# Turning the normed tokens of self-attention in two partition groups, two feature chunks at a time

## The chip, the cores and the metric

The kernel runs on one core of a Trainium2 chip, as one launch. The metric is the device time of that launch in microseconds (us); smaller is better. The core has a matrix engine (TensorE, called PE in the profile, with its weight loads shown as PEld), a vector engine (VectorE, DVE), a scalar engine (ScalarE, ACT), a general engine (GpSimd, POOL) and a queue that issues transfers (SyncE, SP). Each engine works through its own list of instructions in order and waits for the others through semaphores. Matrix products land in PSUM, which is used here in banks of 512 numbers for each of 128 partitions; all other tiles lie in SBUF.

## The reference

One transformer block on 16 batches of 224 tokens with 512 features, all in float32:

```
shift_a, scale_a, gate_a, shift_m, scale_m, gate_m = split(silu(c) @ W_mod + b_mod, 6)
x_norm = ln(x) * (1 + scale_a) + shift_a
q, k, v = split(x_norm @ W_qkv + b_qkv, 3)               # 16 heads of 32 features
x = x + gate_a * (softmax(q k' / sqrt(32)) v @ W_proj + b_proj)
... cross-attention: queries from ln(x), keys and values from ln(context), 750 tokens ...
h = gelu((ln(x) * (1 + scale_m) + shift_m) @ W_mlp1 + b_mlp1)
x = x + gate_m * (h @ W_mlp2 + b_mlp2)
```

The change touches the step from `ln(x)` to `x_norm` in the first line of self-attention. A product contracts over the partitions, so the features of `x_norm` must lie on the partitions, while the normed tokens come with tokens on the partitions. They are turned on PE.

## The kernel before, in words

The kernel runs three stages one after the other: self-attention over all batches, cross-attention, and the MLP. Instructions are emitted in an order written out by hand (class `Ordered` keeps program order on every engine); the tile pools decide which physical buffer a tile gets and put in the waits. All instructions are recorded under line 28, so the profile's groups are told apart by tile names.

Self-attention works on pairs of batches (`PB = 2`, eight pairs p), and in a pair on eight units: four groups g of four heads, for each batch j of the pair. A unit u = 2g + j is a pass of the loop at lines 627 to 642: `self_scores` (products `sc<-qk`, then a DVE maximum `m<-sc` and its split into three bf16 parts, `nm`), the close of an earlier unit (`finish`: DVE reciprocal and product into `at`), planned work of slot 0, `self_weights` of the unit before (`sc<-mrow,ones` and `sc<-qk`, then one ACT exponential into `pt`), `max_rows` (two PE transposes of `nm` and a DVE copy into `mrow`), `add_keys` (a DVE sum `acc`), planned work of slot 1, and `self_values` (`o<-pt,v`, `o<-acc,ones`).

Planned work of pair p prepares pair p + 1. In units 1 and 2 the next pair's tokens are normed (`xn`, written by POOL). Unit 4 holds, in slot 0, the query projection `project_qk(p, 3)` and the turning of chunks 0 and 1; in slot 1, the key projection `project_qk(p, KC + 3)` and the turning of chunks 2 and 3 (lines 551 and 552). Units 5 and 6 hold the value projections of the next pair, unit 7 its first query and key projections. Before the loop, pair 0 is turned by lines 616 and 617. So the turning happens once ahead of the loop and seven times within it.

A chunk k is 128 of the 512 features. `transpose_pair` (lines 310 to 318) turns one chunk of a pair: four transposes, one for each 112 tokens of the 448, into one PSUM bank, then two DVE steps (`modulate`, lines 304 to 308), one for each batch, that multiply and add the per-feature scale and shift while they copy 224 columns from PSUM into `xt`. In a transpose the tokens are the loaded weights and the identity matrix streams past them, so one transpose streams as many columns as it has token rows.

The banks for all of this, for the projections and for `max_rows` come from one pool of three (`ps_mm`, line 234), named `mm` in the profile and handed out in turn. A new tile waits until the last reader of the tile three places earlier is done. In unit 4 the order is: query projection (bank A), chunk 0 (B), chunk 1 (C), `max_rows` (A, free when DVE has moved the query projection out into `qk`), key projection (B, free when chunk 0 is modulated), chunk 2 (C), chunk 3 (A). ACT moves the key projection out.

`Unit.maxima` of cross-attention (lines 1026 to 1046) already turns a tile of 125 rows in two groups of 64 and 61 rows, into two banks; its instructions are called `mm<-ident,top`.

Of the kernel before, what the change touches and what calls it, by code (L numbers as in the profile page):

```python
# [8 lines left out]
F32 = mybir.dt.float32  # L9
# [28 lines left out]
def kernel(  # L38
# [24 lines left out]
    B, N, H = x.shape  # L63
    S = context.shape[1]
    MLP = w_mlp1.shape[1]
    P = 128
    NH = 16
    HD = H // NH
    KC = H // P
    NF = MLP // P  # L70
    HG = P // HD
    TP = 112
    TC = N // TP
    CP = 125
    CC = S // CP
    CH = CC // 2
    RG = 64
    PB = 2
    NP = B // PB
    PT = PB * TC  # L80
    HS = CH * CP
    PN = PB * N
    GB = 4
# [15 lines left out]
    ident = const.tile([P, P], F32, name="ident")  # L99
# [14 lines left out]
    for i in range(3):  # L114
        t = const.tile([TP, TC, HG, HD], BF16, name=f"nm{i}")
# [35 lines left out]
    def load_x(pool, src, bufs):  # L151
        t = pool.tile([TP, TC, H], F32, name="x", bufs=bufs)
        nc.sync.dma_start(out=t, in_=src)
        return t

    def tokens(dram_x, b):
        return dram_x[b].rearrange("(c p) d -> p c d", p=TP)

    def load_w(pool, w, name, bufs=1):
        kc = w.shape[0] // P  # L160
        t = pool.tile([P, kc, w.shape[1]], F32, name=name, bufs=bufs)
        nc.sync.dma_start(out=t, in_=w.rearrange("(k p) n -> p k n", p=P))
        return t

    mm, turn = nc.tensor.matmul, nc.tensor.transpose
# [73 lines left out]
    def load_part(i):  # L239
        w_part[i] = load_w(mp, w_mod[:, i * H : (i + 1) * H], "w_mod", 2)  # L240
# [3 lines left out]
    load_part(0)  # L244
    for b in range(PB):
        xs[b] = load_x(sa, tokens(x, b), 6)
# [8 lines left out]
    for i in range(2):  # L255
        lo = (2 + 3 * i) * H
# [4 lines left out]
    ps = ps_mm.tile([P, 512], F32, name="mm")  # L261
# [15 lines left out]
    def part_rows(i):  # L277

        ps = ps_mm.tile([P, 512], F32, name="mm")
        for k in range(KC):  # L280
            mm(ps[:B, :H], c_t[:, k, :], w_part[i][:, k, :], start=(k == 0), stop=(k == KC - 1))
        if i % 3 < 2:
            r = mp.tile([B, H], F32, name="part", bufs=2)
            nc.scalar.copy(r, ps[:B, :H])
            return r
        return ps
# [17 lines left out]
    def modulate(psum_ap, dst, b, k, i_shift, i_scale):  # L304
        nc.vector.tensor_scalar(
            dst, psum_ap, mod_t[:, i_scale + k, b : b + 1], mod_t[:, i_shift + k, b : b + 1],
            ALU.mult, ALU.add,
        )

    def transpose_pair(pool, psum, xn, p, i_shift, i_scale, k):  # L310

        ps = psum.tile([P, 512], F32, name="mm")
        for t in range(PT):
            turn(ps[:, t * TP : (t + 1) * TP], xn[t // TC][:, t % TC, k * P : (k + 1) * P], ident[:TP, :TP])
        xt = pool.tile([P, PN], F32, name="xt", bufs=2 * KC)
        for j in range(PB):
            modulate(ps[:, j * N : (j + 1) * N], xt[:, j * N : (j + 1) * N], PB * p + j, k, i_shift, i_scale)
        return xt

# [69 lines left out]
    def halves(products):  # L391

        parts = []

        def first():
            parts.append(products())
            next(parts[0])

        return first, lambda: next(parts[0], None)

    def whole(products):
        for _ in products:
            pass
# [32 lines left out]
    if True:  # L436
# [3 lines left out]
        xts = {}  # L440
# [4 lines left out]
        def project_qk(p, m):  # L445
            ps = ps_mm.tile([P, 512], F32, name="mm")
            for k in range(KC):
                mm(
                    ps[:, :PN], (wq, wk)[m // KC][:, k, (m % KC) * P : (m % KC + 1) * P], xts[p][k],
                    start=(k == 0), stop=(k == KC - 1),  # L450
                )
                if k == 1:
                    yield
            t = sa.tile([P, PN], F32, name="qk", bufs=6)
            bm = bcol[:, o_qkv + m : o_qkv + m + 1]
            if m < KC:
                nc.vector.tensor_scalar(t, ps[:, :PN], bm, SCALE, ALU.add, ALU.mult)
            else:
                nc.scalar.activation(t, ps[:, :PN], AF.Identity, bias=bm)
            qk[p, m] = t  # L460
# [12 lines left out]
        def fetch(p):  # L473
            for b in range(PB * p, PB * (p + 1)):
                xs[b] = load_x(sa, tokens(x, b), 6)
# [6 lines left out]
                )  # L482

        def turn_x(p, k):
            xts.setdefault(p, []).append(
                transpose_pair(
                    sa, ps_mm, [xns[PB * p + j] for j in range(PB)], p, i_shift_a, i_scale_a, k
                )
            )

        def project(p, t):
            b, c = PB * p + t // TC, t % TC
            if c == 0:
                gate[b] = gate_rows(sa, 0, b * N, TP, 2)
            ps = ps_mm.tile([P, 512], F32, name="mm")
            yield from project_heads(ps, at[p], wproj, t * TP)
            add_to_x(sa, ps[:TP, :H], xs[b][:, c, :], bproj, gate[b])
            if c == TC - 1:
                nc.sync.dma_start(out=x_self[b], in_=xs[b])
# [3 lines left out]
        def at_slot(p, u, slot, f):  # L503
            if p < NP:
                plan.setdefault((p, u, slot), []).append(f)

        for p in range(NP):
            if p < NP - 1:
                for g in range(1, KC):
                    at_slot(p, 2 * g - 2, 0, lambda p=p, g=g: whole(project_qk(p, g)))  # L510
                    at_slot(p, 2 * g - 2, 1, lambda p=p, g=g: whole(project_qk(p, KC + g)))
                for t in range(PT if p else 0):
                    at_slot(p, 1 + t // 2 * 2, t % 2, lambda p=p, t=t: whole(project(p - 1, t)))
            else:

                left = [(project_qk, p, m) for m in (1, KC + 1, 2, KC + 2)]
                left += [(project, p - 1, t) for t in range(2)]
                left += [(project_qk, p, m) for m in (3, KC + 3)]
                left += [(project, p - 1, t) for t in range(2, PT)]
                parts = [h for f, *args in left for h in halves(lambda f=f, args=args: f(*args))]  # L520
                for i, h in enumerate(parts):
                    at_slot(p, i // 3, i % 3 // 2, h)
            if p == 0:
                made = {}

                def part(i):
                    made[i] = part_rows(i)
                    if i % 3 == 2:
                        finish_part(i, made[i])

                at_slot(p, 1, 0, lambda: part(2))
                at_slot(p, 1, 1, lambda: part(3))
                at_slot(p, 1, 1, lambda: load_part(4))
                at_slot(p, 1, 1, lambda: load_part(5))
                at_slot(p, 2, 0, lambda: finish_part(3, made[3]))
                at_slot(p, 3, 0, lambda: part(4))
                at_slot(p, 3, 1, lambda: part(5))
                at_slot(p, 3, 1, lambda: finish_part(4, made[4]))
                at_slot(p, 3, 1, load_cross)
            n = p + 1  # L540
            if n < NP:
                if n > 1:
                    at_slot(p, 0, 0, lambda n=n: fetch(n))
                at_slot(p, 1, 0, lambda n=n: norm_begin(n))
                for t in range(PT):
                    at_slot(
                        p, 1 + t // 2, t % 2, lambda n=n, t=t: norms[PB * n + t // TC].stats(t % TC)
                    )
                for j in range(PB):
                    at_slot(p, 1 + j, 1, lambda n=n, j=j: norms[PB * n + j].apply())  # L550
                for k in range(KC):
                    at_slot(p, 4, k // 2, lambda n=n, k=k: turn_x(n, k))
                for t in range(PT):
                    at_slot(p, 5 + t // 2, t % 2, lambda n=n, t=t: project_v(n, t))
                at_slot(p, 7, 0, lambda n=n: whole(project_qk(n, 0)))
                at_slot(p, 7, 1, lambda n=n: whole(project_qk(n, KC)))
# [56 lines left out]
        load_part(3)  # L613
        fetch(1)
        wproj = load_w(ws, w_proj, "wproj")
        for k in range(KC):
            turn_x(0, k)
        whole(project_qk(0, 0))
        whole(project_qk(0, KC))
# [213 lines left out]
    with tc.tile_pool(name="ca", bufs=2, reuse_waits="tile") as ca:  # L833
# [3 lines left out]
        xt = {}  # L837
# [94 lines left out]
        for b in range(B):  # L932
            n = b + 1
# [52 lines left out]
        class Unit:  # L986
# [39 lines left out]
            def maxima(self):  # L1026
# [3 lines left out]
                for s in range(HG):  # L1030
                    for c in range(TC):
                        for i, (r, n) in enumerate(((0, RG), (RG, CP - RG))):
                            lo = (s * TC + c) * n
# [3 lines left out]
                            )  # L1037
                for i, n in enumerate((RG, CP - RG)):
                    m = small.tile([TP, HG, TC], F32, name=f"mc{i}")
# [303 lines left out]
```

## Time and profile before

Three runs took 2906.09, 2906.14 and 2911.99 us, median 2906.14. The profiled execution took 2907.9 us.

| what | value |
|---|---|
| profiled execution, own time | 2907.9 us |
| its span, first to last instruction | 2906.1 us |
| granted TensorE clock | 0.993 |
| PE busy | 2834.6 us, 98% |
| DVE busy | 1926.2 us, 66% |
| POOL busy | 1201.5 us, 41% |
| ACT busy | 1119.7 us, 39% |
| self-attention, from 100 to 690 us | PE busy 582.34 of 590 us, DVE 415.71 us |
| transposes `mm<-ident,xn`, 112 rows, all stages | 248, PE busy 30.0 us |
| steps `xt<-mm,mod_t`, 224 columns | 64, DVE busy 28.1 us, 502 ns for one |

PE is busy nearly all the time in every stage, so what counts is what PE has to do and where it stands still. A mean duration in a row covers one instruction from start to end; neighbours overlap, so the step from one to the next is shorter than the duration and is read from the timeline. An idle time in brackets is that of the engine just ahead of the row, with what released it.

### The profile page before, as it was taken

To read this page: it belongs to the slowest core of one execution; us is meant where nothing else is said; L and a number is where in the kernel's file an instruction comes from. 1 tells how busy PE (TensorE), PEld (TensorE's weight loads), DVE (VectorE), ACT (ScalarE), POOL (GpSimd) and SP (SyncE) were. 2 spreads that over 40 slices of the span, in tenths; PEclk is the share of its full clock that TensorE was granted. 3 is DMA by queue.
4 is the path that set the end of the run, shared out by engine and by line. 5 is a ranking of instruction groups with operands and counts; after the bars stand their busy time and mean duration, and the time that the engine had idled before them with its cause. 6 is when DMAs were issued, how large, how long until landed. Compare 5 with 4: busy or idle time off the path is not lost. (4 is left out here: it accounts for less than half of the span.)

```text
span 2906.1 us, 47040 instructions
## 1 busy us (share of the span) xinstructions
PE 2834.6 (98%) x19733; PEld 1810.3 (62%) x19733; DVE 1926.2 (66%) x2764; ACT 1119.7 (39%) x1402; POOL 1201.5 (41%) x1357
## 2 busy tenths in 40 slices
PE   8999999998999999999999999999979999999999
PEld 3444444444555565555656556556546888888888
DVE  4666776676478778787787787877775643444343
ACT  1222222221356655665566556655643112112211
POOL 1022222122356666676666766666551210221021
PEclk9999999998999999999999999999999999999999
DMA  5111110100100010100101100000013111110110
GB/s 191 59 33 33 32 33 10 60 11 24 57 32 24 23 35 24 35 26 21 35 24 35 35 19 28 27 33 24 22 44 107 55 37 37 44 58 29 45 44 30
DMA packets 55384, 114.43 MB, mean 39 GB/s; under 512 B 4308, under 2 KB 4372, under 8 KB 55172
## 3 DMA queue, kind: packets, MB, share of 16 engines
q1 hardware_dynamic: 54560, 110.58, 11.8%
q8 instruction: 155, 2.54, 0.4%
q10 hardware_dynamic: 612, 0.85, 0.1%
q14 instruction: 57, 0.47, 0.1%
HBM read 89.33 MB, written 22.09 MB: 38 GB/s over the span
## 5 line engine op out<-in xcount | busy, mean ns | idle before, releaser
L28 POOL TENSOR_TENSOR acc<-acc,pt 125x448 f32<-125x448 f32 x504 | 573.6, 1138 | 39.5
L28 ACT COPY pt<-sc 125x1792 f32<-125x1792 f32 x192 | 317.3, 1653 | 563.1 <-DVE top L28 510.1
L28 DVE TENSOR_TENSOR pt<-pt,o 125x896 f32<-125x896 f32 x384 | 394.2, 1081 | 88.1 <-PE o L28 85.5
L28 DVE TENSOR_TENSOR top<-top,sc 125x896 f32<-125x896 f32 x320 | 346.4, 1083 | 35.4 <-PE sc L28 28.7
L28 PE MATMUL mm<-wkvc,cxt 128*125 128x512 f32 x768 | 354.4, 604 | 6.9 <-ACT kt L28 6.9
L28 PE MATMUL mm<-cxt,wkvc 128*128 128x375 f32 x1024 | 355.0, 489 | 2.3 <-ACT cxt L28 2.3
L28 ACT ACTIVATE pt<-pt 125x896 f32<-125x896 f32 x384 | 338.4, 951 | 20.0 <-DVE pt L28 19.4
L28 POOL TENSOR_TENSOR upd<-upd,gate 112x512 f32<-112x512 f32 (+1 forms) x60 | 79.2, 1321 | 632.9 <-DVE upd L28 628.4
L28 POOL TENSOR_TENSOR acc<-pt 125x448 f32<-125x448 f32 x126 | 143.8, 1141 | 447.7 <-ACT pt L28 447.7
L28 PEld LDWEIGHTS mm<-cxt,wkvc 128*128 128x128 f32 x1024 | 185.6, 191 | 119.8 <-issue 16.6
L28 DVE RECIPROCAL at<-o 128x224 f32<-128x224 f32 x128 | 198.6, 1552 | 72.9 <-PE o L28 72.9
L28 PEld LDWEIGHTS mm<-wkvc,cxt 128*125 128x125 f32 x768 | 136.5, 187 | 171.5 <-issue 153.2
L28 ACT ACTIVATE pt<-sc 112x1792 f32<-112x1792 f32 x64 | 106.5, 1663 | 333.8 <-PE sc L28 333.8
L28 POOL TENSOR_TENSOR rstd<-mv,eps 112x2 f32<-112x2 f32 (+3 forms) x93 | 18.0, 193 | 508.8 <-DVE mv L28 508.8
L28 PE MATMUL sc<-qt,kt 32*125 32x224 f32 x3072 | 201.6, 377 | 14.0 <-ACT pt L28 13.4
L28 PE MATMUL mm<-xt,wqkv 128*128 128x448 f32 x512 | 208.6, 550 | 5.7 <-DVE xt L28 4.7
L28 DVE TENSOR_REDUCE m<-sc 112x8 f32<-112x1792 f32 x64 | 129.6, 2025 | 121.8 <-PE sc L28 121.8
L28 PEld LDWEIGHTS sc<-qt,kt 32*125 32x125 f32 x3072 | 133.1, 183 | 94.1 <-issue 33.8
L28 PE MATMUL o<-pt,vt 125*32 125x224 f32 x3072 | 158.6, 354 | 0.0
L28 PEld LDWEIGHTS mm<-xt,wqkv 128*128 128x128 f32 x512 | 92.0, 190 | 87.6 <-issue 80.4
L28 DVE TENSOR_REDUCE mc<-mm 112x8 f32<-112x512 f32 (+1 forms) x128 | 79.8, 665 | 98.3 <-PE mm L28 98.3
L28 ACT COPY mx<-a 128x512 f32<-128x512 f32 x26 | 15.2, 586 | 327.0 <-POOL upd L28 307.9
(185 smaller groups left out, 4656.5 us busy)
## 6 DMA issues: line engine op xcount, KB each, us to landing
cx<-in_ctx_dram SPq DMA_DIRECT2D x96, 250.0 KB
x<-in_x_dram SPq DMA_DIRECT2D x16, 448.0 KB
x_self<-x SPq DMA_DIRECT2D x16, 448.0 KB
x<-x_self SPq DMA_DIRECT2D x16, 448.0 KB
x_cross<-x SPq DMA_DIRECT2D x16, 448.0 KB
mx<-x_cross SPq DMA_DIRECT2D x28, 256.0 KB
w<-in_L_xcond_W_mlp_dram SPq DMA_DIRECT2D x7, 1024.0 KB
xr<-x_cross SPq DMA_DIRECT2D x28, 256.0 KB
```

What stands on the lines that cost most here:

```text
L28: return lambda *args, **kw: self.tc.keep_in_program_order(f(*args, **kw))
```

## The change

`transpose_pair` now turns two chunks in one call and takes two banks for it. The 112 token rows are split into partitions 0 to 63 and 64 to 111 (`ROWS`). For each chunk and each 112 tokens there are two transposes, of 64 and of 48 rows, one after the other in the list, into different banks. A bank so holds, for both chunks, the columns of one row group of all four token blocks. The two chunks take 16 transposes instead of eight. Each bank is then modulated in four steps, one for each chunk and batch: eight steps for two chunks instead of four, of 2 x 64 or 2 x 48 columns instead of 224. Each reads a contiguous run from PSUM and writes two separate runs into `xt`. The order of the steps is: chunk k from the first bank (two steps), chunk k from the second bank (two), then chunk k + 1 in the same way. The plan calls the new function once a slot instead of twice; the slots, the pool and the number of banks stay.

```diff
+    ROWS = (0, RG), (RG, TP - RG)
...
+    def turn_rows(banks, srcs, ks):
+
+        for i, k in enumerate(ks):
+            for t, src in enumerate(srcs):
+                for bank, (r, n) in zip(banks, ROWS):
+                    lo = (i * len(srcs) + t) * n
+                    turn(bank[:, lo : lo + n], src[r : r + n, k * P : (k + 1) * P], ident[r : r + n, r : r + n])
+
     def transpose_pair(pool, psum, xn, p, i_shift, i_scale, k):
 
-        ps = psum.tile([P, 512], F32, name="mm")
-        for t in range(PT):
-            turn(ps[:, t * TP : (t + 1) * TP], xn[t // TC][:, t % TC, k * P : (k + 1) * P], ident[:TP, :TP])
-        xt = pool.tile([P, PN], F32, name="xt", bufs=2 * KC)
-        for j in range(PB):
-            modulate(ps[:, j * N : (j + 1) * N], xt[:, j * N : (j + 1) * N], PB * p + j, k, i_shift, i_scale)
-        return xt
+        banks = [psum.tile([P, 512], F32, name="mm") for _ in ROWS]
+        turn_rows(banks, [xn[t // TC][:, t % TC, :] for t in range(PT)], (k, k + 1))
+        xts = []
+        for i in range(2):
+            xt = pool.tile([P, PN], F32, name="xt", bufs=2 * KC)
+            for bank, (r, n) in zip(banks, ROWS):
+                for j in range(PB):
+                    lo = (i * PT + j * TC) * n
+                    modulate(
+                        bank[:, lo : lo + TC * n].rearrange("p (c t) -> p c t", c=TC),
+                        xt[:, j * N : (j + 1) * N].rearrange("p (c t) -> p c t", c=TC)[:, :, r : r + n],
+                        PB * p + j, k + i, i_shift, i_scale,
+                    )
+            xts.append(xt)
+        return xts
...
-            xts.setdefault(p, []).append(
+            xts.setdefault(p, []).extend(
...
-                for k in range(KC):
+                for k in range(0, KC, 2):
                     at_slot(p, 4, k // 2, lambda n=n, k=k: turn_x(n, k))
...
-        for k in range(KC):
+        for k in range(0, KC, 2):
             turn_x(0, k)
```

## The prediction

> **What bounds the kernel now.** I read the page's busy shares first, then the stretches by stage, then who PE waits for, then the timeline around one turn, and at last rows that price the new shapes. Page and stretches (span; PE, PEld, DVE, ACT, POOL busy):
>
> ```profile
> PE 2834.6 (98%) x19733; PEld 1810.3 (62%) x19733; DVE 1926.2 (66%) x2764; ACT 1119.7 (39%) x1402; POOL 1201.5 (41%) x1357
> ...
> 100.00:690.00 590.00, 582.34 (x4515) 287.85 (x4514) 415.71 (x676) 128.95 (x113) 124.16 (x150) 1.00 0.09 27
> ```
>
> In the stage that the change touches PE is busy 98.7% at the full granted clock, DVE 70%. So time moves where PE gets less work or stands longer. What it waits for from 37 to 690 us (total, times, longest):
>
> ```profile
> PE mm L28 <- DVE xt L28: 4.7, 7, 0.7
> PE mm L28 <- DVE qk L28: 3.7, 8, 0.8
> ```
>
> The first comes seven times: once per turned pair, and it ends with a modulate step of just this change. The timeline of the first of the seven (start, length, idle before):
>
> ```profile
> 87.39 0.93 PE L28 MATMUL mm<-ident,xn 112*128 112x112 f32 x8
> ...
> 88.25 0.40 PE L28 MATMUL sc<-mrow,ones 3*112 3x448 bf16 x4
> ...
> 89.10 0.67 DVE L28 TENSOR_SCALAR qk<-mm,bcol 128x448 f32<-128x448 f32 x1
> ...
> 89.69 1.76 DVE L28 TENSOR_SCALAR xt<-mm,mod_t 128x224 f32<-128x224 f32 x4
> 89.83 0.26 PE L28 MATMUL mm<-ident,nm 112*128 112x112 bf16 x2 [0.42 <-DVE qk L28]
> ...
> 90.76 3.25 PE L28 MATMUL mm<-xt,wqkv 128*128 128x448 f32 x8 [0.67 <-DVE xt L28]
> ...
> 93.84 0.93 PE L28 MATMUL mm<-ident,xn 112*128 112x112 f32 x8
> ...
> 94.43 1.77 DVE L28 TENSOR_SCALAR xt<-mm,mod_t 128x224 f32<-128x224 f32 x4 [1.80 <-PE mm L28]
> 94.70 0.96 PE L28 MATMUL o<-pt,v 112*32 112x224 f32 x16
> ```
>
> To see: in unit 4, DVE runs one chain (maximum, reciprocal, `at`, `qk`, four modulates) and PE waits for it twice, 0.42 us for bank A (`qk` moved out) and 0.67 us for bank B (chunk 0 modulated). In slot 0 PE follows DVE, not the reverse. Prices for the new shapes, from cross-attention and the MLP:
>
> ```profile
> 1019.78 0.92 PE L28 MATMUL mm<-xt,wqc 128*128 128x224 f32 x4
> 1020.63 0.66 PE L28 MATMUL mm<-ident,top 64*112 64x64 f32 x16
> 1021.22 0.59 PE L28 MATMUL o<-pt,vt 125*32 125x224 f32 x8
> ...
> 2163.87 1.36 DVE L28 TENSOR_SCALAR mxt<-mm,mod_t 128x128 f32<-128x128 f32 x4
> ```
>
> The row of 16 `top` transposes merges eight of 64 rows with eight of 61: the two-group turn as it already runs. `mxt` is the same modulate on 128 columns.
>
> **The change, step by step.**
>
> *Transposes on PE.* Before, eight take 88.25 - 87.39 = 0.86 us until the next work starts. In two groups, the 16 of `top` take 1021.22 - 1020.63 = 0.59. But they start late: four 224-column products at 1019.78 last 0.92, the last alone 0.35, so a step is 0.19 and they are through at 1020.54; the transposes start at 1020.63, 0.09 later with nothing to wait for in the row. I count that as the price of going from whole-array products to 64-row ones, and get 0.68. Mine load 128 columns against 112; I add 0.01. So 0.69 against 0.86: 0.17 us saved per turn of two chunks. From below: pairs side by side at no entry price, 0.59 (0.27 saved). From above: 16 in series at the present step of (0.93 - 0.26)/7 = 0.096, so 1.53, plus 0.19: 0.86 lost. I take the row of the same instruction.
> The Trainium skill's page "TensorEngine Tiling (Array Packing)" (Key Properties) says that a switch of tiling mode drains TensorE; the 0.09 agrees with it. Its table of theoretical speedup, up to 2x for at most 64 rows, would make it 0.86 to 0.43 and the sum below 1.8 us smaller.
>
> *Modulate steps on DVE.* Four of 224 take 1.76, the last 0.50, so one step is 0.42. Four of 128 take 1.36, the last 0.40: 0.32. By the line through both, 96 columns step 0.285. Mine have 2 x 64 and 2 x 48 columns; that the written run is in two pieces I price at nothing, since `pt<-pt,o` and `top<-top,sc`, both in runs of 224, take 1081 and 1083 ns for 896 elements, the same 1.02 ns each above the 688 ns of a 512-element sum. Eight steps: 4 x 0.32 + 4 x 0.285 = 2.42 against 1.68, 0.74 more DVE time a slot. Bounds: all eight at the 0.22 step of the 32-column rows (below), or every piece priced as a step of its own, 0.50 and 0.47 (above).
>
> *When bank B is free (slot 0).* This is the step that counts. The first bank now holds both chunks, so its last reader is the sixth step, not the second. The start at 89.69 stays: it hangs on DVE's `qk`, and the transposes before it end earlier. Five steps come before the sixth, 0.32 + 0.32 + 0.285 + 0.285 + 0.32 = 1.53, so it starts at 91.22 and, at 0.40 long, ends at 91.62. Before, the second ended at 89.69 + 0.42 + 0.50 = 90.61 and PE started at 90.76, 0.15 later; so now 91.77. The key projection comes 1.01 us later. Queued behind it on PE is everything after.
> The 0.17 saved in slot 0 buys nothing: PE then waits 0.59 instead of 0.42 for `qk`. The same page (PSUM Bottleneck and Gotcha 1) warns that tiling speeds TensorE up but not the emptying of PSUM, and that different row tiles write to different banks; the waits for `qk` and for bank B are where this trace bears on it, and no row before shows the pairing of banks in this turn.
>
> *Slot 1.* Banks C and A are free by 92.6, long before PE gets there. The turn saves its 0.17; its modulates end about 1.05 us later than before and delay the next maximum by as much, but PE has 3.4 us of value projection in between, so `nm` is still ready some 1.4 us before PE asks. `acc` ends near 93.4, asked for at 96.3. ACT, POOL and the transfers keep their order.
> Per pair: 1.01 - 0.17 = 0.84 us; seven pairs: 5.9 us.
>
> *Ahead of the loop.* Here eight modulates (18.26 to 21.69) feed the first query projection (20.12). Now the second transpose of the turn, not the fifth, needs a bank that DVE (`mod_t`) reads until 17.78. From 17.86, 0.1 for the first pair and 0.055 for each of seven more (0.44 from first to last in `top`), and 0.26 until DVE sees the last: the modulates start near 18.56, 0.30 later. The second turn needs the first bank back: sixth step done at 18.56 + 1.93 = 20.49, PE from 20.64, its last transpose at 21.13, DVE from 21.39. The projection follows 0.15 behind the last transpose, as after `top`, at 21.28 instead of 20.12, and its last chunk, due six products or 2.33 later at 23.61, needs the eighth step of the second turn (21.39 + 2.13 + 0.37, and 0.08 for the signal), ready at 23.97. Together 1.16 + 0.36 + 0.07 for the restart: 1.6 us. Nothing later gives it back: the only transfer that PE waits for in the whole trace (`w_mod`, 1.6 us) lies before 17 us; all later waits are for engines that PE itself feeds.
>
> *Sum.* 5.9 + 1.6 = 7.5 us on the span of 2906.1, so 2913.6; with the 1.8 us outside the span the profiled execution would take 2915.4. That execution (2907.9) lies 1.8 above the median 2906.14, so I put the median at 2906.14 + 7.5 = 2913.6, 0.26% slower.
>
> **The rivals.**
>
> *No step is dearer than it looks, and DVE stays ahead (not slower).* One mechanism: bank B is free early enough. It decides where the sixth step ends by 90.78, so that the 0.17 pays for the wait; that means six steps within 1.09 us. The cheapest row of this operation, 32 columns, steps 0.22 and ends at 1.40; even by that a pair loses 0.31, about 2.8 us in all: 2909. With no wait at all, 16 turns save 2.7: 2903.4. Either is within 0.2%, which is about what a measurement of this kernel can tell from no change. A gain above 5.8 us isn't there: all 128 transposes of this stage take some 14 us.
>
> *The delay is given back later.* A wait that ends with a clock of its own, a transfer, would absorb up to 7.5 us: about 2907. Against it: no such wait after 17 us.
>
> *The row groups don't run side by side, or the written pieces cost.* In series slot 1 gains 0.86 + 0.09 instead of -0.17, slot 0's excess hides behind the two waits: 1.96 a pair and some 3 ahead, 2923. With pieces priced as steps the sixth ends 0.84 later: 1.68 a pair and 3 ahead, 2921. Against the first: `top`. The second has no row.
>
> **How the numbers follow.** Forecast (5.8 to 10 us more): 0.58. Dearer than that: 0.13. Below 5.8, by cheaper steps, a smaller entry price or delay given back: 0.25. Faster by more than 0.2%: 0.04, for what I have not seen. So slower 0.71, same 0.25, faster 0.04. The range: below, the cheap steps at 2909 and a point less; above, half way to the dear cases: 2908 to 2919, leaving out about 0.07 on either side.
>
> **What would show it.** In the profile after: PE waits seven times for `xt` at about 1.7 us each instead of 0.67, and some 0.6 instead of 0.42 for `qk`; `mm<-ident,xn` in rows of 64 and 48; `xt` steps of 128 and 96 elements at means near 400 and 366 ns; the period of a pair, 84.54 us before (the row with the 0.67 wait stands at 90.76 and again at 175.30), near 85.4; the MLP unchanged in length. If the wait stays near 0.7, the bank argument is wrong; if it is well over 2 us, the written pieces cost; if the turn of slot 1 takes over 0.86 us, the groups don't overlap.

## The result and the profile after

The changed kernel took 2926.98 us (median of 6 runs, 2915.5 to 2927.4) against 2906.15 us of the kernel before in the same series (6 runs, 2905.51 to 2911.99): a ratio of 1.0056, 95% interval 1.0047 to 1.0066. It is slower, as forecast, but the median lies 8 us above the upper end of the range.

One thing has to be known about the trace of after. Its execution took 2915.5 us (span 2913.7) and was the quickest of the six; the spans of the other five are 2919.6 to 2925.6 us. The forecast for this span was 2913.6. That agreement is an accident, as shown below.

The page of after, busy time by engine, and the stretch from 100 to 690 us (span; PE, PEld, DVE, ACT, POOL busy; clock, share of transfers, GB/s):

```profile
PE 2833.9 (97%) x19861; PEld 1805.9 (62%) x19861; DVE 1937.0 (66%) x2828; ACT 1120.2 (38%) x1402; POOL 1204.0 (41%) x1357
...
100.00:690.00 590.00, 575.57 (x4573) 282.15 (x4565) 421.04 (x726) 126.80 (x111) 122.46 (x148) 1.00 0.10 28
```

PE is busy 0.7 us less in the whole kernel, and in this stretch it stands 14.4 of 590 us where it stood 7.7. What it waits for from 37 to 690 us (total, times, longest):

```profile
PE mm L28 <- DVE xt L28: 11.8, 7, 1.7
PE mm L28 <- DVE qk L28: 4.6, 8, 0.8
```

The total for `xt` went from 4.7 to 11.8 us, for `qk` from 3.7 to 4.6. The timeline of after around the turn that the prediction showed of before (start, length, idle before):

```profile
91.19 0.71 PE L28 MATMUL mm<-ident,xn 64*128 64x64 f32 x16
...
91.83 0.40 PE L28 MATMUL sc<-mrow,ones 3*112 3x448 bf16 x4
...
92.81 0.68 DVE L28 TENSOR_SCALAR qk<-mm,bcol 128x448 f32<-128x448 f32 x1
...
93.40 2.50 DVE L28 TENSOR_SCALAR xt<-mm,mod_t 128x128 f32<-128x128 f32 x8
93.54 0.26 PE L28 MATMUL mm<-ident,nm 112*128 112x112 bf16 x2 [0.55 <-DVE qk L28]
...
95.48 3.25 PE L28 MATMUL mm<-xt,wqkv 128*128 128x448 f32 x8 [1.68 <-DVE xt L28]
```

The order is the one foretold: `qk`, then eight `xt` steps in one chain, and the key projection behind the sixth, 1.68 us idle against 0.67. The groups of the new shapes, each shape apart (busy us, mean ns of one | idle of the engine just before):

```profile
L28 DVE TENSOR_SCALAR xt<-mm,mod_t 128x128 f32<-128x128 f32 x64 | 23.1, 402 | 17.0 <-PE mm L28 17.0
L28 DVE TENSOR_SCALAR xt<-mm,mod_t 128x96 f32<-128x96 f32 x64 | 20.9, 368 | 0.0
L28 PE MATMUL mm<-ident,xn 64*128 64x64 f32 x128 | 12.0, 234 | 0.0
```

So the steps cost what their columns cost (402 and 368 ns; 400 and 366 were forecast), and the two runs that each writes add nothing.

Three marks in the traces show where the time went: the first scores product `sc<-qk` (end of the start), the last transpose of the loop's last turn, and the end. The columns give their times in us and, in brackets, the difference to before. The third kernel is the changed one run again (the run e9 below), a longer execution of the kind that its median stands for.

| mark | before | after, profiled | changed, again |
|---|---|---|---|
| first scores product | 43.47 | 47.17 (+3.7) | 46.37 (+2.9) |
| last transpose of the loop | 601.75 | 611.62 (+9.9) | 618.77 (+17.0) |
| end | 2906.1 | 2913.7 (+7.6) | 2922.6 (+16.5) |

In the profiled execution the loop added 9.9 - 3.7 = 6.2 us, in the other one 14.1 us, with the same waits. The 7.9 us between the two are what the experiments look for.

### The profile page after: what moved, and what is told of

It is laid out like the page before. It is cut to its first block, busy times and chain, and to the rows that moved or that the text cites. A ratio compares the mean times of both kernels' runs of the same rounds, so it can differ in the third digit from the quotient of the medians.

```text
span 2913.7 us, 47358 instructions
## 1 busy us (share of the span) xinstructions
PE 2833.9 (97%) x19861; PEld 1805.9 (62%) x19861; DVE 1937.0 (66%) x2828; ACT 1120.2 (38%) x1402; POOL 1204.0 (41%) x1357
## 3 DMA queue, kind: packets, MB, share of 16 engines
q1 hardware_dynamic: 54560, 110.58, 11.8%
## 5 line engine op out<-in xcount | busy, mean ns | idle before, releaser
L28 PE MATMUL mm<-xt,wqkv 128*128 128x448 f32 x512 | 210.7, 554 | 12.6 <-DVE xt L28 11.8
```

The lines of the kernel that those rows point to most:

```text
L28: return lambda *args, **kw: self.tc.keep_in_program_order(f(*args, **kw))
```

## The experiments

Three theories were set against each other. **A:** the waits alone, as in the prediction; then the profiled execution is the typical one and the high times have some other cause. **B:** the longer waits lower the granted TensorE clock (the share of full speed at which PE's clock runs, 1.00 or 0.50 at any one time in these traces) in most executions, and the lowered clock costs about as much again as the waits. **C:** the transposes in row groups cost something themselves. Each ratio is to the kernel before on the same chip, with its 95% interval.

**e1: the changed kernel again**, to get a trace of another execution. No edit.

> The changed kernel as it is, to get the trace of an execution near the median of 2927 us (the trace at hand is of one with a span of 2913.7). Theory A, the longer waits alone: they cost what the prediction summed, 2.1 us ahead of the loop more than it allowed and 7 x 0.88, so 2914 to 2916, and what lies above has nothing to do with the waits. Theory B, waits and clock: in the trace at hand the granted clock goes in windows of 3.41 us, and it is 0.5 in the window that follows one in which PE was idle for more than half (1.69, 1.74 and above: halved; 1.68 and below: with one exception not). The two waits of unit 4 add up to 0.55 + 1.68 = 2.23 us idle; they fell across a border of windows in the trace at hand, with 1.30, 1.38, 1.47, 1.55, 1.63, 1.68, 1.68 us in the larger part. Where the borders lie otherwise, a pair passes 1.71 and PE runs the next 3.41 us at half speed, which costs up to 1.7 us. B expects a trace of a longer execution to show half-clock windows behind the waits of unit 4, and its time to be the 2913.7 plus 1.7 us for each.

Measured: 2921.12 us against 2910.20, 1.0048 (1.0035 to 1.0060); the trace has a span of 2926.7 us and is that of the longest of its five executions. The waits are the same, 0.55 and 1.68 us a pair, but the granted clock is at a half for one stretch of 3.41 us behind five of the seven waits, and the periods of the pairs go 87.11, 86.82, 85.41, 87.11, 86.86, 85.41 us. A falls, if one more like it shows the same; a third trace (**e9**, no edit, run beside e10 to e12) does.

> The changed kernel once more, so that it stands beside the runs with a busy PE on one chip. Waits alone: 8 us above the kernel before on this chip (0.88 x 7 and 1 to 3 for the start). Waits and clock: 8 us plus up to 1.7 us for each of seven pairs, and a trace whose longer pairs, 86.8 to 87.1 us, are those with a half-clock window behind the wait.

Measured: 2924.31 us against 2908.62, 1.0051 (1.0038 to 1.0065). Its timeline of PE, at the first turned pair and at the third:

```profile
92.73 0.26 PE L28 MATMUL mm<-ident,nm 112*128 112x112 bf16 x2 [0.55 <-DVE qk L28]
...
94.67 4.94 PE L28 MATMUL mm<-xt,wqkv 128*128 128x448 f32 x8 [1.68 <-DVE xt L28]
...
266.68 0.26 PE L28 MATMUL mm<-ident,nm 112*128 112x112 bf16 x2 [0.55 <-DVE qk L28]
...
268.61 3.25 PE L28 MATMUL mm<-xt,wqkv 128*128 128x448 f32 x8 [1.68 <-DVE xt L28]
```

The waits are equal to the hundredth. The eight products behind them take 4.94 us in one place and 3.25 in the other. The stretches around the first, and three whole pairs (the clock is the third figure from the end):

```profile
92.50:95.90 3.40, 1.49 (x6) 0.80 (x6) 3.40 (x11) 1.42 (x1) 0.00 (x0) 1.00 1.05 392
95.90:99.30 3.40, 3.40 (x6) 1.29 (x4) 0.38 (x1) 0.00 (x0) 0.00 (x0) 0.50 1.06 392
99.30:102.70 3.40, 3.40 (x58) 2.19 (x58) 2.41 (x8) 0.64 (x1) 0.00 (x0) 1.00 0.19 67
...
92.70:179.80 87.10, 84.88 (x656) 41.45 (x656) 60.55 (x105) 18.19 (x17) 17.47 (x20) 0.98 0.15 51
179.80:266.70 86.90, 84.63 (x657) 41.56 (x657) 60.16 (x105) 18.27 (x17) 17.48 (x20) 0.98 0.09 27
266.70:352.10 85.40, 83.18 (x657) 40.90 (x657) 60.08 (x105) 18.19 (x17) 17.47 (x20) 1.00 0.10 29
```

In the 3.4 us in which PE is busy for 1.49, the clock is whole; in the next 3.4 it is a half, though PE is busy throughout; then it is whole again. A pair with such a stretch is up to 1.7 us longer, and PE shows as busy for the extra time, so the page's busy share hides the loss. A falls and B stands, as far as traces go. What remained was to move the cause.

**e3: the kernel before with a late bank and no row groups.** One maximum on DVE that nobody reads, about 1.0 us long, ahead of chunk 0's modulates in the loop:

```
+        if p and k == 0:
+            fill = small.tile([P, 7], F32, name="fill", bufs=1)
+            nc.vector.tensor_reduce(fill, ones.unsqueeze(1).to_broadcast([P, 7, P]), AX.X, ALU.max)
```

> The kernel before, with one DVE step more that nothing reads (a maximum over 7 x 128 numbers, about 1.0 us) ahead of the modulates of chunk 0 in the seven turns of the loop: the same late bank by another means, with the whole-row transposes left as they are. Theory A, waits alone: the wait grows from 0.67 to about 1.7, seven times, so 2906.1 + 7 = 2913 at every execution, give or take the 6 us that the kernel before varies by. Theory B, waits and clock: the idle time is 0.42 + 1.7 = 2.1 us a pair, and half-clock windows appear behind the waits wherever the borders let one window hold over half of it: 2913 to 2925, over the 2913 in most executions. A rival C, that the split transposes themselves (more weight loads, changes of row groups) lengthen the changed kernel's executions, expects no half clock here and 2913.

Measured: 2918.44 us against 2910.20, 1.0034 (1.0022 to 1.0047). Waits of PE:

```profile
PE mm L28 <- DVE xt L28: 11.6, 7, 1.7
PE mm L28 <- DVE qk L28: 3.8, 8, 0.8
```

The old turn with the bank 1.0 us late gives the changed kernel's wait, a period of 85.53 us in five pairs, and 87.22 in the one whose clock is halved (from 92.7 us). Behind the loop the trace has six half stretches up to 810 us, as many as before. By time alone this run can't tell A from B; what tells is the half stretch behind a wait. C is not needed: a late bank costs this, whoever makes it late. The run with row groups in the loop alone (e4 below) costs as much on the same chip, 8.4 us against 8.2.

**e6: the same with a shorter maximum** (2 x 128 elements in place of 7 x 128).

> The kernel before with a smaller useless DVE step, a maximum over 2 x 128 numbers (about 0.35 us) ahead of the modulates of chunk 0. Waits alone: the wait grows from 0.67 to about 1.0 us, seven times: 2.4 us above the kernel before. Waits and clock: PE idles 0.42 + 1.0 = 1.4 us a pair; if half of a 3.41 us window is the rule there is no half clock in the loop and the time is the same 2.4 us up; the bank-first run had half clock behind 0.55 + 1.11, so the border may lie lower, and then one or two windows, 2 to 3 us more, are to be seen.

Measured: 2914.73 us against 2910.13, 1.0016 (1.0007 to 1.0025). The common period is 84.87 us, one pair takes 86.56. It lies between, as a dose should: 7 x 0.33 = 2.3 us of waits and one half stretch in the trace.

**e2: the changed kernel with the first bank emptied first**, all four of its steps, then those of the second:

```
-            for bank, (r, n) in zip(banks, ROWS):
+        for bank, (r, n) in zip(banks, ROWS):
+            for i, xt in enumerate(xts):
```

> The changed kernel with the modulate steps in another order: all four of the first bank, then all four of the second. The first bank is then free after four steps of 0.32 us, 0.57 us earlier. Both theories: the wait in unit 4 falls from 1.68 to about 1.11 us, the period of a pair from 85.42 to about 84.85, and the wait ahead of the loop from 1.93 to about 1.36. Theory A, waits alone: 4 us below the changed kernel's median and 0.6 for the start, so near 2922. Theory B, waits and clock: 0.55 + 1.11 = 1.66 us idle never fills half a window, so no half clock in the loop at any place of the borders: span near 2909 to 2911 (2906.1 + 7 x 0.3 + 1 to 3 ahead of the loop), and median 2909 to 2913.

Measured: 2917.38 us against 2910.20, 1.0031 (1.0019 to 1.0042). The wait is 1.11 instead of 1.68 us and the common period 84.85 us, both as they should be when the fourth step releases the bank. Two pairs take 86.39 and 86.35 us, with the clock halved at 262.7 and 518.7; there B had expected none. By time this run does not decide: it lies 3.7 us below e1, where A had expected 4.6, and 7.2 above before, where B's figures come to at most 7. The first of them, and for comparison a place in e1 where the clock was not halved:

```profile
259.20:262.60 3.40, 2.11 (x39) 1.54 (x38) 3.37 (x7) 1.47 (x1) 0.00 (x0) 1.00 0.83 229
262.70:266.10 3.40, 3.13 (x5) 1.52 (x6) 2.44 (x7) 0.09 (x1) 0.00 (x0) 0.50 0.64 185
```

```profile
267.10:270.50 3.40, 1.56 (x6) 0.87 (x6) 3.40 (x11) 1.36 (x1) 0.00 (x0) 1.00 0.82 240
270.50:273.90 3.40, 3.40 (x42) 1.89 (x44) 1.08 (x4) 0.63 (x1) 0.00 (x0) 1.00 0.05 16
```

PE is busy for 2.11 us and the clock drops; it is busy for 1.56 and the clock stays. So no one threshold on the idle time of a stretch fits all places; whether standing still is the cause at all is left to the runs below that take it away (e5, e10).

**e4: the changed turn in the loop only**; pair 0, ahead of the loop, is turned by the old function.

```
+        if p == 0:
+            return [transpose_whole(pool, psum, xn, p, i_shift, i_scale, k + i) for i in range(2)]
```

> The changed kernel, but pair 0, ahead of the loop, is turned the old way. Both theories: the start is that of the kernel before, so the first wait of unit 4 comes some 3.7 us earlier and the half-clock window of 19.1 to 25.9 us is gone. Theory A: 3.7 us below the changed kernel, so 2923 at the median. Theory B: the loop keeps its waits and the borders lie as they come: span 2906.1 + 6.2 = 2912 without half clock in the loop, and up to 12 us more with it.

Measured: 2918.60 us against 2910.20, 1.0037 (1.0024 to 1.0049). From the first transpose to the first scores it takes 26.04 us as before. The loop of its trace has the periods and the five half stretches of e1, so the two traces can be set side by side: 2924.0 us against 2926.7, and 2.7 us is the price of the change ahead of the loop. The medians differ by 2.5, but either kernel's times spread over 10 us.

**e5 and e10: the changed kernel with PE kept busy in the wait.** Two products that nobody reads go to PE between `max_rows` and the key projection, into a free bank of another pool (each shows as two PE instructions, as all products of this size do here). The bank comes as late as before; only PE does not stand still.

```
             row = max_rows(sa, ps_mm, nm)
+            if u == 4 and p < NP - 1:
+                busy = ps_o.tile([P, 512], F32, name="o")
+                for k in range(2):
+                    mm(busy[:, :PN], wq[:, k, :P], xts[p][k], start=True, stop=True)
```

> The changed kernel, with two products more in each of the seven turns' unit 4, right behind the transposes of nm: they write a spare use of the o bank and nobody reads them. They take about 1.5 us of PE, inside the 1.68 us in which it stands and waits for the first bank, so that the time that the waits set stays and only the idleness goes. Theory A, waits alone: no change against the changed kernel, median 2921 to 2927. Theory B, waits and clock: no half-clock window in the loop from 40 to 690 us, the seven pairs at 85.42 us (up to 85.6 if the products end a little late), and the time 2914 to 2919 with what the start and the change of stages lose of the clock, at least 4 us below the changed kernel.

Measured: 2918.45 us against 2910.13, 1.0028 (1.0017 to 1.0039), with no half clock in the loop and every period at 85.42 us. It was run again beside the changed kernel, on one chip:

> The changed kernel with two unread products in the wait for the first bank, as before, beside the changed kernel on the same chip. Waits alone: the same time as the changed kernel. Waits and clock: no half clock in the loop, seven pairs of 85.42 us, and 2 to 10 us less than the changed kernel with a narrower spread.

Measured: 2917.56 us (lowest 2914.49, highest 2918.32), 6.75 us below the changed kernel's 2924.31 of the same chip, with more work on PE. Stretches of e10 by pair, and its timeline at the first wait:

```profile
92.97:178.38 85.41, 84.75 (x660) 41.53 (x660) 60.55 (x105) 18.20 (x17) 17.46 (x20) 1.00 0.16 52
178.38:263.80 85.42, 84.75 (x661) 41.54 (x660) 60.09 (x105) 18.22 (x17) 17.48 (x20) 1.00 0.10 28
263.80:349.21 85.41, 84.75 (x660) 41.52 (x660) 60.10 (x105) 18.20 (x17) 17.49 (x20) 1.00 0.10 29
```

```profile
92.97 0.26 PE L28 MATMUL mm<-ident,nm 112*128 112x112 bf16 x2 [0.54 <-DVE qk L28]
93.07 1.73 PE L28 MATMUL o<-xt,wqkv 128*128 128x448 f32 x4
94.91 2.12 PE L28 MATMUL mm<-xt,wqkv 128*128 128x448 f32 x5
```

This decides between A and B: the key projection starts 1.94 us behind the `nm` transposes as in e9, so the bank comes as late as before, the period is that of a wait at full clock, and the time drops. Two of e9's five executions, 2918.25 and 2918.72 us, were hardly longer than e10's longest; the other three make the difference. What is left of the slowdown, 2917.56 - 2908.62 = 8.9 us, is 7 x 0.88 = 6.2 in the loop and 2.7 ahead of it.

**e11: transposes in place of the products**, 28 of `nm`, also unread, to ask whether transposes keep the clock up too. That would have explained e2, whose stretch with the drop holds many transposes.

```
+        for _ in range(more):
+            turn(ps[:, 512 : 512 + TP], nm[:, 0].rearrange("p s d -> p (s d)"), ident16[:TP, :TP])
```

> The changed kernel with the same wait filled by 28 unread bf16 transposes of nm, some 0.05 us each, 1.4 us in all, into unused columns of their bank, in place of the products. If what the clock goes by is PE's idle time, transposes do as well as products: no half clock in the loop, and the time of the run with the products. If transposes don't count as work for the clock, half-clock windows come behind the waits as in the changed kernel, and its time. This tells whether the 0.7 us of transposes of a turn count with the waits, which would explain half clock behind only 1.28 and 1.35 us of idleness in the bank-first run.

Measured: 2917.62 us, 1.0034 (1.0022 to 1.0047), no half clock in the loop. Whole-row bf16 transposes do it as well. Whether float32 transposes in row groups, as in e2's stretches, count as much was not tested, and those stretches stay open.

**e7: the changed kernel with the first bank on ACT.** Its four steps run on ACT, the second bank's on DVE at the same time:

```
+    def modulate_act(psum_ap, dst, b, k, i_shift, i_scale):
+        nc.scalar.activation(
+            dst, psum_ap, AF.Identity,
+            bias=mod_t[:, i_shift + k, b : b + 1], scale=mod_t[:, i_scale + k, b : b + 1],
+        )
...
+        for bank, (r, n), step in zip(banks, ROWS, (modulate_act, modulate)):
```

> The changed kernel with the four modulate steps of the first bank on ACT, which stands idle there (9.6 us before its exponential), and the four of the second bank on DVE. If the late bank is the whole of the loss, the second wait of unit 4 (1.68 us) goes altogether, and what is left of the change is its shorter transposes: period of a pair 84.54 - 0.67 - 0.12 = 83.75 us, and the start no later than that of the kernel before. Waits and clock: no half clock in the loop. Span 2906.1 - 5.5 = 2900.6, median 2900 to 2906, faster than both kernels. If instead the split transposes cost something that the trace doesn't show, it stays above the kernel before.

Measured: 2905.35 us against 2910.13, 0.9983 (0.9975 to 0.9992). The timeline at the first turn:

```profile
90.90 1.50 ACT L28 ACTIVATE xt<-mm,mod_t 128x128 f32<-128x128 f32 x4 [8.46 <-PE mm L28]
...
92.36 1.23 DVE L28 TENSOR_SCALAR xt<-mm,mod_t 128x96 f32<-128x96 f32 x4
92.49 0.26 PE L28 MATMUL mm<-ident,nm 112*128 112x112 bf16 x2 [0.54 <-DVE qk L28]
92.60 3.24 PE L28 MATMUL mm<-xt,wqkv 128*128 128x448 f32 x8
```

ACT had been idle for 8.46 us and empties the bank before PE asks; the wait for `xt` is gone and the period is 83.58 us, 0.96 under that of before. With both row groups in place and no late bank the loop has no half clock and the kernel is no slower: C falls here as well. One expectation was missed: the start takes 28.25 us, not 26.05 or less, with a half stretch at 20.7.

**e8: the kernel before with its chunks 0 and 2 on ACT**, to see how much of e7 belongs to the row groups: `modulate_act` for even k in the old function.

> The kernel before, whole-row transposes, with the two modulate steps of chunks 0 and 2 on ACT and those of 1 and 3 on DVE. The wait of 0.67 us goes without any split: period of a pair 84.54 - 0.67 = 83.87 us, span 2906.1 - 4.7 = 2901.4, and perhaps 0.5 less ahead of the loop. Against the run with the split and ACT it prices the two-group transposes by themselves: 7 x 0.12 = 0.8 us in the loop in favour of the split.

Measured: 2903.53 us, 0.9977 (0.9968 to 0.9987), period 83.64 us. In the loop whole rows with ACT give nearly the same as row groups with ACT, 83.64 against 83.58 us a pair. Over the whole kernel they are 1.8 us faster, and their start is the shorter one, 25.44 us against 28.25 in e7.

**e12: e8's function ahead of the loop, e7's turn in it.**

> The two gains together: whole-row turns with chunks 0 and 2 on ACT ahead of the loop, two-group turns with the first bank on ACT in the loop. Start as in the kernel before, 26.05 us from the first transpose to the first scores or a little less; pairs of 83.58 us against 83.64 with whole rows and 84.54 before: 7 x 0.96 = 6.7 us under the kernel before, 0.4 under whole rows with ACT, which a measurement can hardly tell.

Measured: 2902.02 us against 2908.62, 0.9980 (0.9971 to 0.9988). It is faster than both kernels, by 6.6 us and by 22 us on this chip, but relative to before not to be told from e8. Its start takes 25.43 us and its pairs 83.58, as expected. The gain is the idle ACT; the row groups bring nothing that shows in the time.

## Why the prediction was wrong

**The direction and its mechanism held.** The bank of the key projection waits for the sixth step, 1.68 us instead of 0.67 ("about 1.7" forecast); for `qk` it is 0.55 ("some 0.6"). The period at full clock is 85.42 us ("near 85.4"), so the loop's own term is 7 x 0.88 = 6.2 us, forecast 5.9. The rival "bank B is free early enough" is out: the wait is there seven times. "Given back later" is out too: e10 keeps 8.9 us to the end. So are dear written pieces (402 and 368 ns); the prediction's price for them at the sixth step, 0.84 us, comes to 0.91 from its own steps, 2.44 - 1.53.

**The saving of a turn was a little smaller.** Forecast 0.69 us for 16 transposes with entry, 0.17 less than before. The timeline of after, the transposes of the second slot and the next work:

```profile
98.65 0.71 PE L28 MATMUL mm<-ident,xn 64*128 64x64 f32 x16
99.30 0.40 PE L28 MATMUL o<-pt,v 112*32 112x224 f32 x4
```

From 98.65 to 99.30 is 0.65 us. The last key product starts at 98.18 and streams for 0.37, so the transposes begin 0.10 late; together 0.75 us, so 0.11 to 0.12 is saved. A pair of transposes steps 0.062 us with 128 weight columns where `top` stepped 0.055 with 112; I had added 0.01 us for all eight pairs together, and it is 0.05. Over seven pairs this accounts for 6.2 against 5.9. The row groups do run side by side: the two transposes of a pair start within 0.02 us of each other. The price that the prediction put on the series was too high, though. Products of 448, 224 and 112 columns step 0.376, 0.19 and 0.096 us, in proportion to their columns, so 64 and 48 columns one after the other would come to about 0.096 a pair, not twice that: an estimate from these rows.
The entry is the place where the Trainium skill's page "TensorEngine Tiling (Array Packing)" (Key Properties) speaks of a drain at a change of mode; the 0.10 us agrees with it, and it takes back half of the 0.21 us that the pairing takes off the transposes.

**The step that failed is the sum, "5.9 + 1.6 = 7.5 us".** Every term of it was priced at the full clock. Behind the wait of 1.68 us, with the 0.55 before it, the clock granted to PE was halved for 3.41 us in five of the seven turns in each of e1, e4 and e9, at up to 1.7 us a time. The loop of e9 lost 14.1 us by the marks, 6.2 of it by the waits and 7.9 by five such stretches, and e10 gave 6.75 us back by keeping PE at work. This term was missing from the sum, from the rivals and from the range. The page of before had the hint: its clock of 0.993 is not 1, and its trace has a half clock behind the long waits of the change of stages (from 697.5 to 714.6 us, and at 796.5). I read the loop's "1.00" and left the clock out.

**Ahead of the loop the price was 2.7 us, not 1.6,** and here too a half clock goes with it. From the first transpose to the first scores it takes 26.05 us before, 28.7 in e1 and e9, and 29.6 in the profiled execution of after, whose stretches are:

```profile
12.00:19.10 7.10, 6.55 (x36) 2.31 (x34) 2.07 (x14) 1.15 (x2) 3.95 (x9) 1.00 1.04 368
19.10:25.90 6.80, 5.13 (x21) 3.02 (x22) 4.61 (x15) 0.00 (x0) 0.00 (x0) 0.50 1.05 388
25.90:40.00 14.10, 14.10 (x35) 6.21 (x35) 0.93 (x3) 1.81 (x3) 0.00 (x0) 1.00 0.69 200
```

Two stretches of 3.41 us run at half clock here, one in e1 and e9, none in before. Every trace whose pair 0 is turned in row groups has such a stretch in its start, and none of the others has. If a half stretch costs its full 1.7 us, the wait for the bank by itself comes to about 1 us (28.7 - 26.05 - 1.7) and the clock to 1.7 or 2.5; no run parted the two.

**Why the profiled span agreed to 0.1 us.** It has 3.7 at the start where I had 1.6, 6.2 in the loop where I had 5.9, no half clock in the loop, and then 2.3 us less than before behind the last turn: four stretches at half clock (712.0 to 725.6) against six in before (five from 697.5, one at 796.5). Too much and too little cancel. The two other executions of the changed kernel with a trace (e1, e9) have a start about 0.9 us cheaper and the loop's loss besides.

That the loop of this execution escaped fits the way the stretches lie. In all these traces the clock changes in steps of 3.41 us, and 25 of them are 85.33 us, while the period of a pair is 85.42. So every wait falls almost on the same place in its stretch as the one before, drifting by 0.08 us a pair. Where a border cuts the two waits, 2.23 us together, neither stretch holds all of it: in the trace of after the larger part was 1.30, 1.38, 1.47, 1.55, 1.63, 1.68 and 1.68 us, and no clock dropped. Where a stretch starts relative to the program differs from trace to trace. That the place of the stretches decides is argued from the traces; no run set it on purpose.

That the clock is what parts the six executions (2915.5 to 2927.4 us) can be read from the clock listed for each: 0.993 at a span of 2913.7 us, 0.991 at 2919.6, 0.988 or 0.989 at 2925.0 to 2925.6. The time lost by the clock, its missing share times the span, is 20.4, 26.3 and, at 2925.6, 32.2 us. It grows by 5.9 and 11.8 us where the span grows by 5.9 and 11.9; one execution, 2925.0 us at 0.988, lies further off with 35.1, and three digits of the clock leave 1.5 us open in each. So the measured median is that of executions which lost some 12 us more by the clock than the profiled one.

The Trainium skill's page "TensorE: Matmul & The Clock Gate" describes this gate: half clock or full, judged in free-running windows of 3413 ns (Part 1), which agrees with the 3.41 us steps here. Its rule, no idle gaps over about 3.4 us (HAM oscillation), does not: by it no wait of this change could have cost any clock, and waits of 0.55 and 1.68 us did (e9, against e10, where the second is filled). The measurement decides.

**What stays open** is the rule by which a stretch is judged. In e1 1.8 us of idle time in a stretch left the clock alone at two places (267.1 and 526.6), in e2 1.3 us dropped it at two (259.2 and 515.2). What a stretch holds seems to matter. Of the loop's stretches (their borders taken from the changes of the clock) with 1.0 us or more of idle time, those that hold only five to eight PE instructions part cleanly: the next stretch was at half clock in all ten with 1.84 us or more, and in none of the 21 with 1.80 or less, over seven traces. Those that hold 28 to 39, score products on 32 rows among them, were followed by half clock behind 1.27 us (e2) and not behind 1.42 (e3). No run varied this by itself.

## What to carry to other kernels

A wait on PE can have two prices: its own length, and, where two short waits fall close together as here, a stretch at half clock behind them; the second shows as busy time, so look for it in the clock of narrow windows, and price a new wait with and without it. When one bank takes over the work of two, ask which step releases it and empty it in that order, or give it to an engine that is idle then: here four steps on ACT were worth more than the whole rearrangement of the transposes. One profiled execution that agrees with a sum proves little; see that the terms agree, mark by mark.

## What the hardware showed that was not expected

- About 2 us of waiting in 3.4 us, in two pieces of 0.55 and 1.68, can be followed by a half clock in the next 3.41 us, and that came back in five of seven turns: 7.9 us in e9, over a quarter of a per cent of the kernel.
- Unread work in the wait takes the half clock out of the loop: two 448-column products (1.73 us) or 28 bf16 transposes (30 with the two of `max_rows`, 1.64 us), 2917.56 and 2917.62 us against 2924.31.
- A transpose pair in two row groups steps 0.062 us with 128 weight columns and 0.055 with 112.
- ACT applies a scale and a shift for each partition from PSUM at a price near DVE's: four of 128 columns in 1.50 us (e7; DVE 1.36 for `mxt` in before), two of 224 in 0.96 (e8; DVE 0.92).
